# Edge weights of a graph layer: one 128-row product a tile with a zero-padded map, in place of pairs of 64-row products

## The chip, the cores and the metric

One Trainium2 chip, one of its cores. The metric is the device time of one launch in microseconds (us); lower is better. TensorE (PE) does the matrix products and its weight loads (PEld), VectorE (DVE) and ScalarE (ACT) the elementwise work, GpSimd (POOL) issues the gathers, SyncE (SP) issues loads and stores.

## The reference, cut to what matters

A graph layer with 12,500 nodes of 160 numbers (64 scalars and 32 vectors of 3) and 400,000 edges sorted by their target node. The part around the change:

```python
hid = jax.nn.silu(edge_scalars @ fc_w1 * _inv(R))      # (400000, 64) @ (64, 64)
w = hid @ fc_w2 * _inv(FC_HID)                         # (400000, 64) @ (64, 224)
w1, w2, w3, w4, w5 = jnp.split(w, [64, 128, 160, 192], axis=-1)
es, ev = h_s[edge_src], h_v[edge_src]                  # gather by source node
m_s1 = w1 * es * e0
m_v1 = (w2 * es)[:, :, None] * e1[:, None, :]          # and three more products
agg = jax.ops.segment_sum(mid, edge_dst, num_segments=n) * inv_nn
```

Every edge thus gets 224 weights from its 64 hidden numbers, these multiply the gathered source node, and the results are summed over the edges of each target. Two linear maps, a gate, a residual and a layer norm over the nodes follow. All is float32.

## The kernel before, in words

A first stage writes the mapped nodes to a table in HBM (`h_tab`) and prepares constants. Then the edges are taken in tiles of 128: 3125 tiles, in chunks of 20. The ten first tiles of a chunk lie on partitions 0 to 63 of the loaded edge data `es`, the ten others on partitions 64 to 127; the code calls these the two halves. `quads` cuts a chunk into five steps of four tiles, two of each half, so that there are 782 steps in all.

The main loop (L607 to L631) is unrolled, and its order on each engine is the order in which the program is written. One step n does this:

- `hide(n + 1)` (L608): in three steps of five, PE makes the hidden layer of the next tiles with a block-diagonal 128x128 map (L290), and ACT applies the SiLU (L292). The rows of `hid` again hold the two halves.
- `gather` (L299): POOL issues four indirect DMAs, one a tile, into a tile `hg`, of which there are four.
- `weights` (L311): PE makes the 224 weights of each of the four tiles into `pw`, with the tile's slice of `hid` as the stationary and `w2` as the moving operand. A tile of half 0 uses rows 0 to 63 of both, one of half 1 rows 64 to 127, and the loop takes them alternately.
- `products` (L319, and L328 three times): DVE multiplies `pw` by `hg` into `pr`, of which there are two.
- `add_up` and `add` (L387): DVE adds an earlier block's result into the accumulator. `choose` (L338, L341): DVE builds a selection tile every 1.25 steps.
- `go_on` does one piece of the finishing work on nodes that are complete (L394 to L437; the transposes L406 are PE's).
- `now`: pieces kept from the step before, either four transposes (L369) with two copies by ACT (L370), or eleven products (L378) with one copy (L382).
- `sum_up` of step n - 1 (L357): PE sums its `pr` by target, 16 products of 128x32 stationary columns, four side by side on the columns of the array. When two blocks are full, ACT copies them out (L361).

A product in float32 appears as two MATMUL records, each with its own weight load, so the four products of `weights` are eight records. PE signals DVE, ACT and SP through one semaphore, which the last record of each group raises. `w2` is built in the first stage: L235 to L242.

```python
    w2 = consts.tile([2 * S, NWT], F32, name="w2")
...
        for t in sorted(range(n), key=lambda t: (slots[t][1], slots[t][0])):
            half, c = slots[t]
            r = slice(half * S, (half + 1) * S)
            nc.tensor.matmul(pw[:, t, :NWT], hid[r, c * P:(c + 1) * P], w2[r],
                             start=True, stop=True)
```

Of the kernel before, what the change touches and what calls it, by code (L numbers as in the profile page):

```python
# [10 lines left out]
F32 = mybir.dt.float32  # L11
# [9 lines left out]
P = 128  # L21
S = 64
# [14 lines left out]
NWT = 224  # L37
# [19 lines left out]
def place_of(part, piece):  # L57

    first, step, count = SUMS[part]
    at = [first + a * step[0] + b * step[1] for a in range(count[0]) for b in range(count[1])]  # L60
    return at.index(PIECE[piece])
# [3 lines left out]
def gnn_kernel(  # L65
# [21 lines left out]
    nc = tc.nc  # L87
# [8 lines left out]
    consts = ctx.enter_context(tc.tile_pool(name="consts", bufs=1))  # L96
# [12 lines left out]
    for i in range(2):  # L109
        r = slice(S + i * V, S + (i + 1) * V)  # L110
# [31 lines left out]
    with tc.tile_pool(name="nodes", bufs=2) as nodes, tc.tile_pool(  # L142
        name="nodes_ps", bufs=8, space=PSUM
    ) as nps:
        CH = 4 * U * P
        for c0 in range(0, N, CH):
# [13 lines left out]
            for u in range(-(-cq // P)):  # L160
# [4 lines left out]
                for q in range(quarters):  # L165
                    r = slice(q * V, (q + 1) * V)
# [3 lines left out]
            for q in range(quarters):  # L170
                t = c0 // P + q * U
# [5 lines left out]
            if cn > full * P:  # L177
                n = cn - full * P
                t = c0 // P + full
# [52 lines left out]

    w1 = block_diagonal("w1", fc_w1, 2, 1.0)

    w2 = consts.tile([2 * S, NWT], F32, name="w2")  # L235
    for half in range(2):
        r = slice(half * S, (half + 1) * S)
        at_c = 0
        for c0, c1 in ((64, 128), (0, 64), (192, 224), (160, 192), (128, 160)):
            nc.scalar.dma_start(w2[r, at_c:at_c + c1 - c0], fc_w2[:, c0:c1])  # L240
            at_c += c1 - c0
    nc.vector.tensor_scalar_mul(w2, w2, 1.0 / math.sqrt(64))  # L242

# [19 lines left out]
    for to, part, pieces, w, r0, c0, by in maps:  # L263
        for k, piece in enumerate(pieces):
            half, at_p = divmod(place_of(part, piece), 3)
            m = terms.setdefault((to, part, half), len(terms))
            at_r = at_p * V
            r = l2[at_r:at_r + V, m, c0:c0 + w.shape[1]]
# [32 lines left out]
                in_offset=bass.IndirectOffsetOnAxis(ap=i, axis=0))  # L301
        return hg

    def weights(psum, hid, slots):

        pw = psum.tile([P, Q, 256], F32, name="pw")
        n = len(slots)
        for t in sorted(range(n), key=lambda t: (slots[t][1], slots[t][0])):
            half, c = slots[t]
            r = slice(half * S, (half + 1) * S)  # L310
            nc.tensor.matmul(pw[:, t, :NWT], hid[r, c * P:(c + 1) * P], w2[r],  # L311
                             start=True, stop=True)
        return pw

    def products(pool, pw, hg, n, between=()):

        pr = pool.tile([P, Q, NPR], F32, name="pr")

        nc.vector.tensor_mul(  # L319
            pr[:, :n, 6 * V:10 * V].rearrange("p t (k c) -> p t k c", k=2),  # L320
            pw[:, :n, :2 * S].rearrange("p t (k c) -> p t k c", k=2),
            hg[:, :n, None, :S].to_broadcast([P, n, 2, S]))
        for f in between:
            f()

        for k, (first, step) in enumerate(((1, 2), (4, -2), (10, 1))):
            full = pr[:, :n, first * V:]
            nc.vector.tensor_mul(  # L328
                bass.AP(tensor=full.tensor, offset=full.offset,
                        ap=[full.ap[0], full.ap[1], [step * V, 3], [1, V]]),  # L330
                pw[:, :n, None, 2 * S + k * V:2 * S + (k + 1) * V].to_broadcast([P, n, 3, V]),
                hg[:, :n, S:].rearrange("p t (i c) -> p t i c", i=3))
        return pr
# [51 lines left out]
    def add(base, os, b):  # L385
        window = acc[:, :, ds(base, W)]
        nc.vector.tensor_add(window, window, os[:, :, b])  # L387
# [66 lines left out]
    with tc.tile_pool(  # L454
        name="fin", bufs=1
    ) as fin, tc.tile_pool(name="edge", bufs=2) as edge, tc.tile_pool(
        name="deep", bufs=4
    ) as deep, tc.tile_pool(name="pw_ps", bufs=2, space=PSUM) as pw_ps, tc.tile_pool(
        name="pa_ps", bufs=2, space=PSUM
# [13 lines left out]
        def index(t):  # L473
            return group(t // GT)[0][:, t % GT:t % GT + 1]


        chunks = [((c, SIDE), (c + SIDE, SIDE)) for c in range(0, NB * TB - 2 * SIDE + 1, 2 * SIDE)]
# [8 lines left out]
        ess, hids = {}, {}  # L486

        def hide(n):

            if n >= len(steps):  # L490
                return
            c, i, _ = steps[n]
            if i % 2:
                return
            edges = [(t * P, m) for t, m in chunks[c]]
            if i == 0:
                ess[c] = load_hidden(loads, edges)
            hids[c, i // 2] = hidden(edge, misc_ps, ess[c], edges, 2 * i, 4)
# [104 lines left out]
        with tc.manual_schedule(engines={ENG.PE, ENG.DVE, ENG.Activation, ENG.Pool}):  # L603
            hide(0)
            before = None
            pieces = list(range(0, N, CHN))
            for n, (c, i, tiles) in enumerate(steps):  # L607
                hide(n + 1)  # L608
                hg = gather(deep, [index(t) for t, _, _ in tiles])
                now, later = later, []  # L610
                pw = weights(pw_ps, hids[c, i // 2], [(half, u - i // 2 * 4) for _, half, u in tiles])
                ready = []
                pr = products(edge, pw, hg, len(tiles), [lambda: ready.extend(add_up(1))])
                for a in ready:
                    add(*a)

                need = [b for m, b in order if m <= n]
                todo = [b for _, b in order if b not in sels]
                for b in need:
                    choose(b)  # L620
                order = [(m, b) for m, b in order if b not in need]
                if not need and order and order[0][0] <= n + 2:
                    choose(order.pop(0)[1])
                go_on()
                for f in now:
                    f()
                if before is not None:
                    sum_up(*before)
                before = (tiles, pr)
                if n % 30 == 6 and pieces:  # L630
                    self_connection(pieces.pop(0))  # L631
            assert not pieces
            sum_up(*before)
            while later:
                later.pop(0)()
            while adds:
                for a in add_up(1):
                    add(*a)
            while doing or to_do:
                go_on()  # L640
# [4 lines left out]
        with tc.For_i(0, n_redo, 1):  # L645
            n_again = nc.values_load(again[0:1, 0:1], min_val=0, max_val=G)
            sides = [(0, 3), (3, 2)]
            with tc.For_i(0, n_again, 1) as g, tc.For_i(0, BG, 1) as k:
                b = g * BG + k
                idx = loads.tile([P, TB], I32, name="idx1", bufs=1)  # L650
                nc.sync.dma_start(idx, src[ds(g, 1), :, ds(k * TB, TB)].rearrange("o p t -> p (o t)"))
                eat = loads.tile([P, TB, 4], F32, name="eat1", bufs=1)
                nc.sync.dma_start(eat, ea[ds(g, 1), :, ds(k * TB, TB)].rearrange("o p t k -> p (o t) k"))
                ends = loads.tile([1, 2], I32, name="ends1", bufs=1)
                nc.sync.dma_start(ends, bounds[:, ds(b, 1)].rearrange("k o -> o k"))
                edges = [(b * EB + t * P, m) for t, m in sides]
                es = load_hidden(loads, edges)
                hid = hidden(edge, misc_ps, es, edges, 0, 4)
                prs = {}
                for slots in quads([m for _, m in sides]):  # L660
                    hg = gather(deep, [idx[:, sides[h][0] + u:sides[h][0] + u + 1] for h, u in slots])
                    pr = products(edge, weights(pw_ps, hid, slots), hg, len(slots))
                    for slot, (h, u) in enumerate(slots):
                        prs[sides[h][0] + u] = pr[:, slot]
                r = edge.tile([P, TB], F32, name="r", bufs=1)
                nc.vector.tensor_scalar_add(r, rel[:, ds(b * TB, TB)], -float(W))
                first = nc.values_load(ends[0:1, 0:1], min_val=0, max_val=N - 1)
                last = nc.values_load(ends[0:1, 1:2], min_val=0, max_val=N - 1)
                with tc.For_i(first + W, last + 1, W) as base:
                    base = nc.s_assert_within(  # L670
                        base, 0, N - 1, skip_runtime_bounds_check_because="it is at most `last`")
                    sel = select(edge, r, eat)
                    pa = cleared(pa_ps)
                    for t in range(TB):
                        add_tile(pa[:, 0], sel, t, prs[t], start=False, stop=(t == TB - 1))
                    tt = edge.tile([V3, 2, 4, NO, W], F32, name="tt", bufs=1)
                    turned(misc_ps, copied(edge, pa, 1), 1, tt, 0)
                    add(base, second(edge, misc_ps, tt, 1), 0)
                    nc.vector.tensor_scalar_add(r, r, -float(W))
            for job in jobs:  # L680
                for f in finish(fin, misc_ps, *job):
                    f()
# [46 lines left out]
```

## Time and profile before

| what | us |
|---|---|
| median of 3 runs | 5778.92 (5755.6 to 5812.79) |
| the profiled execution | 5669.53 |
| its span, first to last instruction | 5667.7 |
| PE busy | 4182.8 (74%) |
| POOL busy | 3051.9 (54%) |
| DVE busy | 2642.3 (47%) |
| PEld busy | 2227.6 (39%) |
| ACT busy | 809.3 (14%) |
| mean granted TensorE clock | 0.816 of full |

The main loop runs from 114.9 us to 5626 us and looks the same in every slice. PE's busy time is no measure of full use: the ends of its matmuls are modelled and contain the latency of each. An idle engine is told in the profile by what ended its idle time ("<-"); "issue" means that no wait is seen, "remote" that a semaphore was awaited whose source the profile could not place.

### The profile page before, as it was taken

Reading aid. Unit: us, or ns where it says so; the run is one execution under the profiler, and the core shown is the slowest. Engines: PE = TensorE matmul, PEld = TensorE weight load, DVE = VectorE, ACT = ScalarE, POOL = GpSimd, SP = SyncE. Lnnn points to the kernel's source line nnn. Section 1 sums busy time; section 2 is a strip of 40 time slices with the busy share of each in tenths; the row PEclk is TensorE's granted clock in tenths of the full one; section 3 lists DMA queues with packets and bytes.
Section 4 is the critical chain, followed back from the end, with each engine's and each line's share of the span. In section 5 each row is a group of like instructions: output and inputs, shape, how many; then the busy total and the mean of one; then the engine's idle time right before and its main releaser. Section 6 shows DMA issues by size and latency. Waiting matters only on the chain.

```text
span 5667.7 us, 89792 instructions
## 1 busy us (share of the span) xinstructions
PE 4182.8 (74%) x36179; PEld 2227.6 (39%) x36179; DVE 2642.3 (47%) x5628; ACT 809.3 (14%) x1639; POOL 3051.9 (54%) x3134
## 2 busy tenths in 40 slices
PE   6777777767777767777777777777776767777776
PEld 5334433333344434334333333433333433434343
DVE  4444444444444444444444444444444444444444
ACT  0111111111111111111111111111111111111111
POOL 3555555555555555555555555555555555555553
PEclk7788887888888878888888788887887888888787
DMA  6222222222222222222222222222222322232221
GB/s 172 68 72 73 72 72 66 73 74 65 76 76 67 74 68 74 74 70 74 72 74 73 63 76 69 73 77 68 75 72 63 82 67 73 71 79 69 68 69 46
DMA packets 232392, 416.39 MB, mean 73 GB/s; under 512 B 64580, under 2 KB 160592, under 8 KB 231713
## 3 DMA queue, kind: packets, MB, share of 16 engines
q0 software_dynamic: 150000, 256.20, 17.3%
q1 hardware_dynamic: 65972, 142.43, 9.9%
q10 hardware_dynamic: 15994, 11.93, 0.8%
q8 instruction: 285, 4.67, 0.3%
q14 instruction: 141, 1.16, 0.1%
HBM read 394.32 MB, written 16.00 MB: 72 GB/s over the span
## 4 chain that ended last, share of the span: by engine, by line
PE 31%; another core or an unknown queue 8%; issue 6%; DVE 3%; ACT 3%; DVEq 0%; DMA 0%; POOL 0%; ACTq 0%; POOLq 0%
PE pa L357 13%; PE pw L311 6%; PE ph L290 4%; PE po L378 3%; PE pt L369 2%; DVE pr L328 2%; ACT tt L370 1%; PE pa L348 1%; ACT hid L292 1%; DVE pr L319 0%; PE pp L406 0%; PE psc L510 0%; ACT L292 0%; DVEq L582 0%
## 5 line engine op out<-in xcount | busy, mean ns | idle before, releaser
L299 POOL DMA_INDIRECT hg<-h_tab,idx x3125 | 3029.5, 969 | 2562.8 <-DVE pr L328 962.0
L357 PE MATMUL pa<-pr,sel 128*32 128x192 f32 x25000 | 1813.8, 395 | 312.7 <-issue 298.8
L319 DVE TENSOR_TENSOR pr<-pw,hg 128x512 f32<-128x512 f32 x782 | 539.1, 689 | 2648.7 <-remote 1400.2
L357 PEld LDWEIGHTS pa<-pr,sel 128*32 128x32 f32 x25000 | 888.3, 127 | 1060.3 <-issue 768.8
L328 DVE TENSOR_TENSOR pr<-pw,hg 128x384 f32<-128x384 f32 x2346 | 1158.2, 549 | 5.7 <-issue 4.9
L311 PE MATMUL pw<-w,hid 64*128 64x224 f32 x6250 | 990.0, 429 | 48.3 <-issue 38.8
L369 PE MATMUL pt<-ident,sa 128*96 128x128 f32 x1250 | 317.8, 344 | 814.6 <-ACT tt L370 418.6
L311 PEld LDWEIGHTS pw<-w,hid 64*128 64x128 f32 x6250 | 645.2, 219 | 585.8 <-issue 530.2
L341 DVE TENSOR_TENSOR sel<-oh,eat 128x640 f32<-128x640 f32 x625 | 517.8, 828 | 168.2 <-PE pw L311 51.2
L290 PE MATMUL ph<-es,w 128*128 128x512 f32 x940 | 552.0, 673 | 10.8 <-issue 8.3
L369 PEld LDWEIGHTS pt<-ident,sa 128*96 128x96 f32 x1250 | 124.7, 144 | 1000.5 <-ACT tt L370 496.0
L361 ACT COPY sa<-pa 128x384 f32<-128x384 f32 x313 | 149.5, 478 | 2085.0 <-PE pa L357 1042.7
L292 ACT ACTIVATE hid<-ph 128x512 f32<-128x512 f32 (+1 forms) x470 | 247.0, 526 | 1242.9 <-PE ph L290 855.1
L378 PE MATMUL po<-tt,l 96*96 96x256 f32 (+1 forms) x1738 | 401.7, 383 | 9.6 <-issue 8.7
L378 PEld LDWEIGHTS po<-tt,l 96*96 96x96 f32 x1738 | 274.5, 164 | 127.1 <-issue 47.6
L370 ACT COPY tt<-pt 96x256 f32<-96x256 f32 x626 | 229.3, 366 | 588.0 <-PE pt L369 361.1
L290 PEld LDWEIGHTS ph<-es,w 128*128 128x128 f32 x940 | 165.8, 219 | 198.1 <-issue 184.7
L406 PE MATMUL pp<-ident,acc 96*128 96x96 f32 x196 | 44.9, 325 | 239.6 <-DVE acc L387 218.9
L338 DVE TENSOR_TENSOR oh<-rel,iota 128x160 f32<-128x160 int16 x625 | 196.3, 314 | 0.0
L382 ACT COPY os<-po 96x512 f32<-96x512 f32 (+1 forms) x79 | 45.6, 577 | 714.9 <-PE po L378 485.1
L387 DVE TENSOR_TENSOR acc<-acc,os 96x64 f32 x625 | 132.7, 212 | 12.6 <-ACT os L382 7.9
L406 PEld LDWEIGHTS pp<-ident,acc 96*128 96x128 f32 x196 | 23.8, 170 | 273.3 <-issue 187.5
(61 smaller groups left out, 794.7 us busy)
## 6 DMA issues: line engine op xcount, KB each, us to landing
es<-in_es_t_dram SPq DMA_DIRECT2D x312, 320.0 KB
hg<-h_tab,idx POOLq DMA_INDIRECT x3125
h_tab<-ht ACTq DMA_DIRECT2D x8, 960.0 KB
xt<-in_x_dram SPq DMA_DIRECT2D x24, 320.0 KB
out_dram<-y SPq DMA_DIRECT2D x24, 320.0 KB
eat<-in_ea_dram SPq DMA_DIRECT2D x25, 250.0 KB
xv<-in_xv_t_dram SPq DMA_DIRECT2D x25, 187.5 KB
xs<-in_xs_t_dram SPq DMA_DIRECT2D x25, 125.0 KB
```

Source lines behind the costliest of these rows:

```text
L290: nc.tensor.matmul(ph[:k, c], w1[:k, :k], es[:k, t0 * P + c0 * P:t0 * P + c1 * P], start=True, stop=True)
L292: nc.scalar.activation(hid[:k, c], ph[:k, c], AF.Silu, scale=1.0 / math.sqrt(64))
L299: nc.gpsimd.indirect_dma_start(out=hg[:, t, :], out_offset=None, in_=h_tab, in_offset=bass.IndirectOffsetOnAxis(ap=i, axis=0))
L311: nc.tensor.matmul(pw[:, t, :NWT], hid[r, c * P:(c + 1) * P], w2[r], start=True, stop=True)
L319: nc.vector.tensor_mul(pr[:, :n, 6 * V:10 * V].rearrange("p t (k c) -> p t k c", k=2), pw[:, :n, :2 * S].rearrange("p t (k c) -> p t k c", ...
L328: nc.vector.tensor_mul(bass.AP(tensor=full.tensor, offset=full.offset, ap=[full.ap[0], full.ap[1], [step * V, 3], [1, V]]), pw[:, :n, None ...
L338: nc.vector.tensor_tensor(oh, r[:, :, None].to_broadcast([P, TB, W]), iota[:, None, :].to_broadcast([P, TB, W]), op=OP.is_equal)
L341: nc.vector.tensor_mul(sel, oh[:, :, None, :].to_broadcast([P, TB, 4, W]), e[:, :, :, None].to_broadcast([P, TB, 4, W]))
L357: nc.tensor.matmul(pa[k * W:(k + 1) * W], sel[:, t, k], a, start=start, stop=stop)
L369: nc.tensor.transpose(pt[:, half, b], sa[:, b, half * V3:(half + 1) * V3], ident)
L370: nc.scalar.copy(tt[:, half, :, at_b:at_b + nb].rearrange("c k b n -> c b k n"), pt[:, half, :nb].rearrange("c b (k n) -> c b k n", k=4))
L378: nc.tensor.matmul(po[:, k, :nb], l2[:, terms[to, part, half]], tt[:, half, part, :nb], start=(n == 0), stop=(n == len(of) - 1))
```

## The change

`w2` becomes two maps side by side, each of 128 rows: in the first, rows 64 to 127 are zero, in the second rows 0 to 63. Each tile's product now takes all 128 rows of its `hid` slice, both halves, against the map in which the other half's rows are zero. In the last chunk, where a column of `hid` has only half 0, it takes rows 0 to 63. The number of instructions in the main loop, their order, and what they wait for are the same on all five engines; the setup gains one memset and its scaling covers 448 columns in place of 224.

```diff
-    w2 = consts.tile([2 * S, NWT], F32, name="w2")
+    w2 = consts.tile([2 * S, 2, NWT], F32, name="w2")
+    nc.vector.memset(w2, 0.0)
     for half in range(2):
         r = slice(half * S, (half + 1) * S)
...
-            nc.scalar.dma_start(w2[r, at_c:at_c + c1 - c0], fc_w2[:, c0:c1])
+            nc.scalar.dma_start(w2[r, half, at_c:at_c + c1 - c0], fc_w2[:, c0:c1])
...
-    def weights(psum, hid, slots):
+    def weights(psum, hid, slots, filled):
...
-            r = slice(half * S, (half + 1) * S)
-            nc.tensor.matmul(pw[:, t, :NWT], hid[r, c * P:(c + 1) * P], w2[r],
+            r = slice(0, 2 * S) if c < filled else slice(0, S)
+            nc.tensor.matmul(pw[:, t, :NWT], hid[r, c * P:(c + 1) * P], w2[r, half],
                              start=True, stop=True)
...
-                pw = weights(pw_ps, hids[c, i // 2], [(half, u - i // 2 * 4) for _, half, u in tiles])
+                pw = weights(pw_ps, hids[c, i // 2], [(half, u - i // 2 * 4) for _, half, u in tiles],
+                             chunks[c][1][1] - i // 2 * 4)
...
-                    pr = products(edge, weights(pw_ps, hid, slots), hg, len(slots))
+                    pr = products(edge, weights(pw_ps, hid, slots, 2), hg, len(slots))
```

## The prediction

> **What bounds the kernel now.** I read the page's busy lines first, then the costliest groups, then the waits, then the timeline of one stretch. No engine is full: POOL 54%, DVE 47%. PE shows 74%, but that holds latencies. The span less the first stage, (5626 - 115) / 782, is 7.05 us a step. A step of POOL alone is four gathers at 0.95 us and 0.30 between them, 5.0 us; of DVE 2642.3 / 782 = 3.4 us. So the loop is bound by engines waiting in turn, and the question is whether `pw` (L311) lies in that ring. From the page's groups and from the waits:
>
> ```profile
> L299 POOL DMA_INDIRECT hg<-h_tab,idx x3125 | 3029.5, 969 | 2562.8 <-DVE pr L328 962.0
> L319 DVE TENSOR_TENSOR pr<-pw,hg 128x512 f32<-128x512 f32 x782 | 539.1, 689 | 2648.7 <-remote 1400.2
> L311 PE MATMUL pw<-w,hid 64*128 64x224 f32 x6250 | 990.0, 429 | 48.3 <-issue 38.8
> L369 PE MATMUL pt<-ident,sa 128*96 128x128 f32 x1250 | 317.8, 344 | 814.6 <-ACT tt L370 418.6
> ```
>
> ```profile
> DVE pr L319 <- remote: 1400.2, 267, 19.1
> POOL hg L299 <- DVE pr L328: 962.0, 291, 7.6
> DVE pr L319 <- PE pw L311: 784.7, 285, 10.1
> DVE pr L319 <- PE pa L357: 260.4, 51, 8.2
> ```
>
> Nearly all of DVE's idle time stands before L319, and L319 waits for the gathers, for `pw`, and through PE's semaphore for the release of a `pr`. POOL in turn waits for DVE to give an `hg` back. The timeline shows which is late:
>
> ```profile
> 3034.50 1.32 POOL L299 DMA_INDIRECT hg<-h_tab,idx  x1 [0.30 <-issue]
> 3035.16 1.03 PE L311 MATMUL pw<-w,hid 64*128 64x224 f32 x8
> 3036.12 4.99 PE L378 MATMUL po<-tt,l 96*96 96x256 f32 x22
> 3039.88 0.95 POOL L299 DMA_INDIRECT hg<-h_tab,idx  x1 [0.30 <-issue]
> 3041.43 0.69 DVE L319 TENSOR_TENSOR pr<-pw,hg 128x512 f32<-128x512 f32 x1 [5.48 <-PE po L378]
> ...
> 3043.90 1.03 PE L311 MATMUL pw<-w,hid 64*128 64x224 f32 x8
> 3044.86 0.53 PE L357 MATMUL pa<-pr,sel 128*32 128x192 f32 x8
> 3044.97 0.69 DVE L319 TENSOR_TENSOR pr<-pw,hg 128x512 f32<-128x512 f32 x1 [0.73 <-PE pw L311]
> ```
>
> The reader is to see two kinds of step. At 3043.90 the products start as the last pass of `pw` ends: `pw` is the late one. At 3035.16 `pw` ends at 3036.19, its gathers landed before, and DVE still waits 5.2 us: PE's semaphore arrives late. Followed step by step over the trace (start of L319 less end of the last L311), 274 of 781 steps start within 0.25 us of the end, 148 within 0.25 to 1.25 us, and 359 later. The late ones have a pattern: they come while POOL issues gathers and just after a dense burst of PE records. With POOL idle around it no PE signal is late; after the 32 records of L357 and then L311, with POOL busy, four of five are, by 2 to 4 us on average; after L290, which puts two records into 1 us, about one in ten. It behaves like a backlog that drains slowly. I don't know what it is, only when it comes.
>
> **What the skill says.** "TensorE: Matmul & The Clock Gate", Part 3, says that products of small contraction on different row groups run at the same time, and that one with few rows takes as long as one with all. The trace agrees:
>
> ```profile
> 3026.39 1.86 PE L311 MATMUL pw<-w,hid 64*128 64x224 f32 x8
> 3029.70 1.12 PE L290 MATMUL ph<-es,w 128*128 128x512 f32 x2
> 3030.76 1.03 PE L311 MATMUL pw<-w,hid 64*128 64x224 f32 x8
> 3036.12 4.99 PE L378 MATMUL po<-tt,l 96*96 96x256 f32 x22
> ```
>
> L378 runs one pass after the other: (4.99 - 0.38 for the last) / 21 = 0.219 us for 256 columns, or 0.19 us for 224. Eight passes of L311 in single file would take 8 x 0.19 = 1.52 us and an end of 0.27; 1.03 us is 4 x 0.19 + 0.27. The pairs do overlap fully. "TensorEngine Tiling (Array Packing)", Key Properties, says that a change of tiling drains the array. The trace agrees in kind: the L290 at 3029.70 has two 512-column passes, 2 x 0.43 = 0.86 us, and L311 starts 1.06 us after it, so 0.2 us is lost to the first weight load and the change of shape. The forecast goes by both.
>
> **The change part by part.**
>
> *Single file.* Each step's `pw` gains 4 x 0.19 = 0.75 us at full clock. The granted clock here is either full or half. At half, L311 takes 1.86 us at 3026.39, and the gain is 1.5. The passes run from 346 to 741 ns with median 349 and mean 429, so (429 - 349) / 349 = 23% of them are at half clock. Mean: 0.77 x 0.75 + 0.23 x 1.5 = 0.92 us; over 781 steps 720 us of PE time.
>
> *Shape changes.* `pw` now has the full-row shape of L290 before it in 469 steps (938 passes of L290, two a group), and of L369 or L378 after it in 313 + 79 steps. There the weights can load under the product before and nothing drains: bounded by 0 and 0.2 us a boundary; I take 0.2 before and 0.15 after, 94 + 59 = 150 us. The changes to and from L357 stay. Net PE time: 570 us, and 720 if nothing is saved.
>
> *Records.* Eight MATMUL and eight loads as before, in twice the time. No new wait on any queue, and none queued behind one; DVE, ACT, POOL and SP get the same lists.
>
> *Setup.* One memset of 128x448 on DVE: a memset of 96x1056 takes 0.94 us in the trace, so 0.4 us, at about 1.5 us, where DVE next waits for DMAs (idle 2.9 us). ACT's loads of `w2` start at 35 us, long after. The scaling grows from 0.25 to about 0.5 us at 63 us, before a DVE wait of 5.7 us for a DMA. Taken as nothing; without that cover, under 1 us.
>
> *How much of the 570 is on the path.* This is where I choose. Low bound: in a step whose signal is late by more than the gain, DVE starts when the backlog has drained, and a `pw` that takes longer with the same number of records gives it time to drain, so DVE sees nothing. Taking in every step only what the gain exceeds the lateness gives 336 of a gross 749 us (each step at its own clock), 45%. High bound: the chain. In the stretch from 3000 to 3060 us it runs through PE most of the time (L357 32.1%, L311 18.0%, L290 9.5%), because PE's own order puts L357, L290 and the next `pw` behind this one; then nearly all is exposed. PE does have slack: 814.6 us before L369 and 239.6 before L406. I take 55%: 570 x 0.55 = 315 us. What hides the rest is the late signal; were it gone, all 570 would show.
>
> *Clock.* A full-row pass works twice as many rows. Over the trace's 3.4 us clock stretches, the clock drops to half after those with little array work (columns x rows x stationary columns) and returns after those with much; the level between, about 2650 of 8192 full-clock array cycles, sorts some 95% of them. With the work of `pw` doubled in place, the stretches above it rise from 63% to 70%: 0.07 x 5510 = 386 us of time would go from half to full clock. That saves up to half of what PE works in it; at 0.35 us per us and 55% exposed, some 70 us. Bounds: 0 and 135.
>
> Sum: 315 - 70 = +245 us. On the profiled execution 5669.5 + 245 = 5915 us. The median of the three runs lies 109 us (1.9%) above that execution, so I put the same increment on the median: 5779 + 245 = 6024, stated as 6020.
>
> **The rivals.**
>
> - *PE is the whole path (0.20).* Everything adds: 570 to 720 us, centre 6350. For it: the chain. Against it: the 814.6 us of PE idle before L369 and the 359 late steps.
> - *Absorbed (0.14).* The extra passes lie in the time that DVE waits for late signals and POOL for buffers: within 1%, 5780. For it: DVE's 1400.2 us of "remote". Against: 274 steps have no lateness at all.
> - *The clock carries it (0.15), on the other side.* If the denser array holds the full clock nearly throughout, each of the some 185 half-clock steps gets back 1.1 us on L357 (2.3 against 1.2 us of starts for its 32 passes), 0.8 on the old `pw` and some 0.5 on the rest, 2.4 us or 440 us; 70% exposed it is -310 us, against a cost that then has no half-clock part, 0.55 x (781 x 0.75 - 150) = 240: 70 us faster, 5710. It decides where the mean granted clock passes about 0.93. Against it: the in-place count gives 70% of stretches, or 0.85.
> - *The change does not do what it says:* if full-row passes still overlapped, the time would fall by the 150 us of boundaries. L378 and L290 go in single file, so I give this nothing of its own; the rival before it holds its range.
>
> **How the numbers follow.** The likeliest case, partly exposed, has 0.51; its own range is +110 to +400 us, 5890 to 6180. Slower by over 1% is that case and the first rival, 0.71; within 1% (about what a measurement of this kernel can tell from no change) 0.14; faster 0.15. The range leaves out half of the faster case and the upper end of the first rival: 5730 to 6330.
>
> **What would show it.** After: L313 in 128*128 form, eight passes in about 1.78 us at full clock; its start about 0.86 us after a 512-column L291 at full clock; L321's idle time with "PE pw" growing by about 0.3 us a step and "remote" shrinking; POOL's wait for L330 growing by about the added time; clock 0.83 to 0.86. Wrong if `pw` groups stay near 1.03 us, if the clock goes over 0.93, or if "remote" falls by far more than the growth in "PE pw", which would mean that late signals hang on the shape of `pw` and not on the burst before it.

## The result, and the profile after

| kernel | median, us | runs | profiled execution, us | mean granted clock |
|---|---|---|---|---|
| before | 5785.34 (5755.6 to 5817.4) | 20 | 5669.53 | 0.816 |
| after | 5805.97 (5790.48 to 5828.53) | 20 | 5798.33 | 0.870 |

The ratio is 1.0034, 95% interval 1.0018 to 1.0051: 10 to 30 us slower, where 245 us were forecast. The likeliest case was wrong; what came is, for the larger part, the rival "Absorbed". The groups of `pw` take longer, as was expected; the rest of PE's work gets shorter at the higher clock, and of what remains hardly anything shows in the time.

The two profiles can't be laid side by side as they are: the profiled execution of before lay 2% under its own median, that of after lay on it. The 129 us between the spans are therefore not the change. The page of after, busy times and groups:

```profile
PE 4414.6 (76%) x36179; PEld 2830.2 (49%) x36179; DVE 2649.1 (46%) x5629; ACT 807.5 (14%) x1639; POOL 3050.2 (53%) x3134
...
L300 POOL DMA_INDIRECT hg<-h_tab,idx x3125 | 3027.8, 969 | 2690.8 <-DVE pr L330 1073.5
L359 PE MATMUL pa<-pr,sel 128*32 128x192 f32 x25000 | 1679.4, 377 | 282.0 <-issue 276.7
L321 DVE TENSOR_TENSOR pr<-pw,hg 128x512 f32<-128x512 f32 x782 | 540.0, 691 | 2796.2 <-remote 1372.0
L313 PE MATMUL pw<-w,hid 128*128 128x224 f32 x6250 | 1490.5, 384 | 34.0 <-issue 28.1
...
L371 PE MATMUL pt<-ident,sa 128*96 128x128 f32 x1250 | 296.8, 325 | 752.1 <-ACT tt L372 432.7
```

and its waits:

```profile
DVE pr L321 <- remote: 1372.0, 234, 19.3
...
POOL hg L300 <- DVE pr L330: 1073.5, 307, 8.7
...
DVE pr L321 <- PE pw L313: 879.1, 336, 11.2
```

L313 is in its 128-row form and its busy time half as long again; each wait shown and each row of another engine stands within some 12% of its partner of before. PE's busy time as a whole grows by less than L313 does, by 232 us, from 4182.8; one of the rows that shrank is L359, whose partner of before was

```profile
L357 PE MATMUL pa<-pr,sel 128*32 128x192 f32 x25000 | 1813.8, 395 | 312.7 <-issue 298.8
```

Two steps from the timeline of after:

```profile
3032.95 1.68 PE L313 MATMUL pw<-w,hid 128*128 128x224 f32 x8
...
3034.66 0.69 DVE L321 TENSOR_TENSOR pr<-pw,hg 128x512 f32<-128x512 f32 x1 [2.01 <-PE pw L313]
...
3036.39 1.12 PE L291 MATMUL ph<-es,w 128*128 128x512 f32 x2
...
3037.35 1.68 PE L313 MATMUL pw<-w,hid 128*128 128x224 f32 x8
...
3044.55 0.69 DVE L321 TENSOR_TENSOR pr<-pw,hg 128x512 f32<-128x512 f32 x1 [6.41 <-remote]
```

The group takes 1.68 us instead of 1.03. In the first step DVE starts 0.03 us after the group's end, so in this step all of the longer group is on DVE's path. In the second the group ends at 3039.03 and DVE starts 5.5 us later; there DVE can hardly see 0.65 us more or less at PE. L313 starts 0.96 us after L291, where its partner started 1.06 us after L290. Step by step over the trace, 354 of 781 steps start within 0.25 us of the end of `pw` (before 274) and 326 later than 1.25 us (before 359).

The runs below were made in five sets, each with its own runs of the kernel before, and that kernel took 4218 and 4222 us in the first and the last set and 5660, 5787 and 5788 us in the three between; so ratios hold within a set only. What differs in the traces is the subject of the experiments: in the first and last set no PE semaphore that could be matched to its group came later than 0.2 us after the group's end ("on time"), in the sets between, and in both profiles above, many did ("late"; their lateness sums to some 4400 us over the trace of before and 4500 us over that of after, as far as the signals, of which some 5% are missing from these two traces, can be matched to their groups).

### The profile page after: what moved, and what is told of

It is laid out like the page before. It is cut to its first block, busy times and chain, and to the rows that moved or that the text cites. A ratio compares the mean times of both kernels' runs of the same rounds, so it can differ in the third digit from the quotient of the medians.

```text
span 5796.5 us, 89793 instructions
## 1 busy us (share of the span) xinstructions
PE 4414.6 (76%) x36179; PEld 2830.2 (49%) x36179; DVE 2649.1 (46%) x5629; ACT 807.5 (14%) x1639; POOL 3050.2 (53%) x3134
## 4 chain that ended last, share of the span: by engine, by line
PE 34%; another core or an unknown queue 8%; issue 4%; ACT 3%; DVE 2%; DVEq 0%; DMA 0%; ACTq 0%
PE pa L359 13%; PE pw L313 10%; PE ph L291 4%; PE po L380 3%; PE pt L371 2%; DVE pr L330 1%; ACT tt L372 1%; ACT hid L293 1%; PE pa L350 1%; ACT sa L363 0%; PE psc L512 0%; PE pp L408 0%; ACT L293 0%; DVE pr L321 0%
## 5 line engine op out<-in xcount | busy, mean ns | idle before, releaser
L300 POOL DMA_INDIRECT hg<-h_tab,idx x3125 | 3027.8, 969 | 2690.8 <-DVE pr L330 1073.5
L359 PE MATMUL pa<-pr,sel 128*32 128x192 f32 x25000 | 1679.4, 377 | 282.0 <-issue 276.7
L321 DVE TENSOR_TENSOR pr<-pw,hg 128x512 f32<-128x512 f32 x782 | 540.0, 691 | 2796.2 <-remote 1372.0
L313 PE MATMUL pw<-w,hid 128*128 128x224 f32 x6250 | 1490.5, 384 | 34.0 <-issue 28.1
L313 PEld LDWEIGHTS pw<-w,hid 128*128 128x128 f32 x6250 | 1276.8, 209 | 393.3 <-issue 347.2
L359 PEld LDWEIGHTS pa<-pr,sel 128*32 128x32 f32 x25000 | 846.1, 122 | 934.0 <-issue 696.0
L330 DVE TENSOR_TENSOR pr<-pw,hg 128x384 f32<-128x384 f32 x2346 | 1159.9, 550 | 6.2 <-issue 5.4
L371 PE MATMUL pt<-ident,sa 128*96 128x128 f32 x1250 | 296.8, 325 | 752.1 <-ACT tt L372 432.7
L291 PE MATMUL ph<-es,w 128*128 128x512 f32 x940 | 529.9, 647 | 12.4 <-issue 7.4
L380 PE MATMUL po<-tt,l 96*96 96x256 f32 (+1 forms) x1738 | 396.5, 378 | 17.9 <-issue 16.7
L380 PEld LDWEIGHTS po<-tt,l 96*96 96x96 f32 x1738 | 278.8, 163 | 114.0 <-issue 33.8
L291 PEld LDWEIGHTS ph<-es,w 128*128 128x128 f32 x940 | 161.4, 213 | 196.8 <-issue 183.2
```

The source lines that it names most:

```text
L291: nc.tensor.matmul(ph[:k, c], w1[:k, :k], es[:k, t0 * P + c0 * P:t0 * P + c1 * P], start=True, stop=True)
L300: nc.gpsimd.indirect_dma_start(out=hg[:, t, :], out_offset=None, in_=h_tab, in_offset=bass.IndirectOffsetOnAxis(ap=i, axis=0))
L321: nc.vector.tensor_mul(pr[:, :n, 6 * V:10 * V].rearrange("p t (k c) -> p t k c", k=2), pw[:, :n, :2 * S].rearrange("p t (k c) -> p t k c", ...
L330: nc.vector.tensor_mul(bass.AP(tensor=full.tensor, offset=full.offset, ap=[full.ap[0], full.ap[1], [step * V, 3], [1, V]]), pw[:, :n, None ...
L359: nc.tensor.matmul(pa[k * W:(k + 1) * W], sel[:, t, k], a, start=start, stop=stop)
L371: nc.tensor.transpose(pt[:, half, b], sa[:, b, half * V3:(half + 1) * V3], ident)
```

## The experiments

**The products of a half in turn.** The sort now puts the two products of one half next to each other. It was made to take the pairs apart without a change of shape.

```diff
-        for t in sorted(range(n), key=lambda t: (slots[t][1], slots[t][0])):
+        for t in sorted(range(n), key=lambda t: (slots[t][0], slots[t][1])):
```

> The kernel before with the two tiles of half 0 ahead of the two of half 1, so that the 64-row products go in single file and hardly overlap, with no zero rows, no denser array and no change of shape saved. Theory 1 (absorbed: the time is set by late PE signals during the gathers, and the longer edge weights lie beside): within 1% of before, 5730 to 5840 us. Theory 2 (cancelled: the longer PE time costs some 250 us or more, and the changed kernel gets it back from the clock and the shape changes): 6030 to 6190 us. In both, a group of eight passes takes about 1.6 to 1.7 us at full clock and the granted clock stays near 0.82.

Measured, on time: 4221.29 us against 4218.03, ratio 1.0004 [0.9992, 1.0016]. But its timeline shows that the premise failed:

```profile
3032.90 1.03 PE L311 MATMUL pw<-w,hid 64*128 64x224 f32 x8
```

The group still takes 1.03 us. The eight passes start in pairs, 13 ns apart (7 ns before), the pairs 183 to 293 ns apart, though two products of one half now follow each other in the program. So PE seems to have taken up the other half's products ahead of them (the trace shows neither the half of a pass nor the order in which the passes were queued; in program order the group would take some 1.5 us, an estimate: six gaps of 0.19 us and the last pass's 0.35 us). This run therefore says nothing about single file, and is in effect a second profile of the kernel before, with signals on time; its groups:

```profile
L299 POOL DMA_INDIRECT hg<-h_tab,idx x3125 | 3069.6, 982 | 1092.1 <-issue 973.3
...
L319 DVE TENSOR_TENSOR pr<-pw,hg 128x512 f32<-128x512 f32 x782 | 539.3, 690 | 1390.8 <-DMA hg<-h_tab,idx 789.2
```

POOL issues its gathers back to back ("issue", mostly the 0.30 us between two, is 973.3 of its 1092.1 us of idle time), 3125 of them 1.25 us apart, 3.9 ms of the 4.2. With signals on time the gathers are the pace.

The same kernel in a late set:

> The kernel of halves_in_turn once more, since its first run fell where PE's signals are on time and the gathers set the pace (before 4218 us). If the signals are late this time (before near 5660 to 5790 us): theory 1 (the longer weights lie beside late signals) says within 1% of before; theory 2 (cost cancelled by the denser array's higher clock, which this kernel lacks) says 4 to 7% slower. If they are on time again: ratio 1.000, as before.

5791.25 us against 5787.13, 1.0002 [0.9983, 1.0021], groups of 1.03 us again. It serves below as a profile of the old form whose span (5779.6 us) does lie at its median.

**The change twice over, to see where PE becomes the bound.** Every product of the changed kernel is made twice into the same place, eight more passes or 1.5 us a step.

```diff
-            nc.tensor.matmul(pw[:, t, :NWT], hid[r, c * P:(c + 1) * P], w2[r, half],
-                             start=True, stop=True)
+            for _ in range(2):
+                nc.tensor.matmul(pw[:, t, :NWT], hid[r, c * P:(c + 1) * P], w2[r, half],
+                                 start=True, stop=True)
```

> The changed kernel with each edge-weight product issued twice (the second overwrites the first with the same values): 1.5 us of full-row PE work more in each step, 32 PE records in place of 16. Theory 1: up to 150 us more than the changed kernel, at most 5950 us, since PE's own work at full clock, about 6 us a step, still fits into the 7.05 us. Theory 2: 0.55 x 781 x 1.5 = 640 us more less some 100 us for the clock, about 6350 us.

On time: 5309.21 us, 1.2584 [1.2564, 1.2603], and nearly the whole idle time of the products is `pw`:

```profile
DVE pr L322 <- PE pw L314: 2437.5, 775, 15.0
```

PE is busy for 93% of the span at a clock of 0.968: with the gathers no longer the pace, PE is. (Neither range of the expectation, made for late signals, applies here.)

> The kernel of full_twice once more. With signals on time it took 5309 us, 1.258 of before, PE 93% busy. With late signals: theory 1 says that 1.5 us of PE work more a step is again partly beside, and the dense burst before the signal is followed by a longer, sparser stretch, so it loses much less than 26%: 1.00 to 1.10 of before, at most 6300 us. Theory 2: 1.10 to 1.15 and up.

Late: 6063.24 us, 1.0474 [1.0439, 1.0509]. Eight more passes at 0.19 us are 781 x 1.51 = 1180 us; the clock rises from 0.865 to 0.944 and shortens other work, so that PE's busy time grows by 817 us (4420.0 in `after_third`, 5236.8 here). The time rises by 265 us over the 5798.43 us of the changed kernel in the same set. Where PE's signals are late, two thirds of even this are not seen.

**The weights one step ahead.** `pw` of step n + 1 is made before the products of step n wait, so that DVE finds it ready; once with pairs, once with full rows.

```diff
-                hide(n + 1)
+                hide(n + 2)
...
-                pw = weights(pw_ps, hids[c, i // 2], [(half, u - i // 2 * 4) for _, half, u in tiles])
+                pw, pws[n + 1] = pws.pop(n), weigh(n + 1)
```

> The kernel before with the edge weights and the hidden layer made one step earlier, so that PE's signal for a step's weights is one step old when DVE needs it. Nothing is left out. Theory 1: lateness of that signal no longer holds DVE, and the time falls well below before, to some 4800 us (as a bound, the 1530 us that DVE waits for weights that are already made would go: 4250). Theory 2: PE's own order is the path, and the time stays within 3% of before, 5600 to 5950 us.

> The changed kernel with the same shift by one step as in the run ahead_pairs. Theory 1: as fast as ahead_pairs within 2% as long as the gathers set the pace; slower than it by up to 400 us (0.5 us of PE a step) if PE sets it. Theory 2: within 1% of ahead_pairs, as the cost and the clock cancel there as well.

On time: 4184.28 us, 0.9922 [0.9905, 0.9940], and 4187.93 us, 0.9924 [0.9907, 0.9940]. With `pw` made a step ahead, full rows and pairs cost the same, and both gain 0.8%. The signals being on time, these two runs say nothing about what lateness costs. In a late set:

> The kernel of ahead_full once more (changed kernel, weights one step earlier). With signals on time it took 0.992 of before. With late signals: theory 1 says that the lateness of the weights' own signal is taken off DVE, some 1000 us or more, 4600 to 5000 us where before takes 5700; theory 2 says no more than 3% off.

5675.53 us, 0.9824 [0.9789, 0.9860]: a gain, but not the one expected. DVE hardly waits for `pw` any more (120.8 us are left) and instead waits for other late signals:

```profile
DVE pr L321 <- remote: 1009.5, 206, 19.4
...
DVE pr L321 <- PE pa L359: 616.0, 187, 9.0
```

**Both kernels again, unchanged.**

> The kernel before itself, for a trace beside that of the changed kernel in the same condition: ratio 1.00. If PE signals are on time, DVE's waits before L319 are for the landing of gathers and not 'remote', POOL's starts are 1.25 us apart nearly throughout, and no step has a signal later than 0.2 us; if they are late, the picture of the first profile, near 5785 us.

> The changed kernel itself once more, to have it beside a run of the kernel before whose PE signals are on time (before took 4218 us in the runs of the first set, with no late PE signal in their traces, against 5785 us where its own profile was taken). Theory 1, now: the pace is set beside PE, by POOL's gathers where the signals are on time (4 x 1.25 us a step, 3.94 ms in all) and by the late signals where they are not, so the changed kernel is within 0.7% of before in either condition. Theory 2 (cost cancelled by the clock): with the signals on time the clock is higher before the change already (0.91 in the run with the halves in turn), little is left to gain, and the PE time shows: 3 to 6% slower, 4340 to 4470 us where before takes 4218.

> The changed kernel a third time. Late signals: ratio 1.003, as twice before. Signals on time: theory 1 says within 0.7% of before, because four gathers take 5.0 us a step and PE's work with full rows about as much; theory 2 says 3 to 6% slower.

Before against itself 0.9991 [0.9975, 1.0007]; after 1.0035 [1.0013, 1.0057] and 1.0018 [1.0006, 1.0030]. The change costs 0.2 to 0.4% in late sets. The set on time that the expectation of `after_again` hoped for did not come.

**One gather in four.** POOL gathers only the first tile of each step, and the products of all four read it: three quarters of the gathered data are left out. DVE and PE do as much as before.

```diff
-        for t, i in enumerate(idx):
+        for t, i in enumerate(idx[:1]):
...
-            hg[:, :n, None, :S].to_broadcast([P, n, 2, S]))
+            hg[:, :1, None, :S].to_broadcast([P, n, 2, S]))
...
-                hg[:, :n, S:].rearrange("p t (i c) -> p t i c", i=3))
+                hg[:, :1, S:].rearrange("p t (i c) -> p t i c", i=3).to_broadcast([P, n, 3, V]))
```

> The kernel before with one gather a step in place of four; all four tiles are multiplied by the first tile's rows, so three quarters of the gathered data are left out. POOL then needs 1.25 us a step. Theory 1: the gathers were the pace, so the time falls, to what DVE and PE need: 3.4 us a step of DVE, some 4 us of PE, 3200 to 3600 us. Theory 2: PE is the path already, and the time falls by less than 5%.

> The changed kernel with one gather a step in place of four, as in one_gather_pairs. Theory 1: with the gathers out of the way PE is the path and the price of the single file shows: 250 to 500 us slower than one_gather_pairs. Theory 2: equal to one_gather_pairs within 1.5%, since clock and shape changes pay for it there as well.

In a set where before took 5659.88 us: pairs 3741.88 us, 0.6616 [0.6597, 0.6636], longer than the 3200 to 3600 us expected; full rows 4130.04 us, 0.7296 [0.7274, 0.7318]. Two things follow. The late signals go: one of the nearly 3000 matched PE semaphores comes later than 0.5 us. And the change now costs 388 us, 0.50 us a step. The wait of the products for `pw` with pairs,

```profile
DVE pr L319 <- PE pw L311: 887.4, 549, 5.9
```

and with full rows:

```profile
DVE pr L321 <- PE pw L313: 1275.4, 724, 12.3
```

The difference of these two lines, 388.0 us, is the difference of the times. Here, and only here, is DVE's wait for `pw` the change's price one for one; PE is busy for 89 and 90% of these spans.

**Single file without full rows.** To replace the run whose premise had failed: all four products take rows 0 to 63.

```diff
-            r = slice(half * S, (half + 1) * S)
+            r = slice(0, S)
```

> All four products of a step take rows 0 to 63 (the weights of the second half's tiles are computed from the first half's hidden numbers, so a part of the computation is changed), so no two can run side by side: the eight passes go in single file as in the changed kernel, while the rows worked and the change of tile shape at every boundary stay as before. First, the group is 1.6 to 1.8 us at full clock against 1.03, or the premise fails. Absorbed (the longer weights lie in time that is lost anyway): within 0.5% of before, clock 0.80 to 0.83. Paid by the clock (single file costs, and the higher clock of the full rows gives it back): slower than before by 1.5 to 5%, at a clock of 0.80 to 0.83, while the changed kernel was at 1.003. If the set has signals on time, where before takes 4218 us, absorbed gives within 0.5% as well.

> The same single file of 64 rows, with one gather in four (three quarters of the gathered data left out), where PE sets the pace and every step's price shows. The pairs took 3741.88 us and the full rows 4130.04 us. If single file alone is the price, 781 steps at 0.65 us give +508 us: 4250 us, and the changed shape and clock then give 120 us back in the full-row form. If the boundaries give nothing back, about 4130 us; if they give back the 150 us that the forecast took, about 4280 us.

Both fell into a set with signals on time. `same_rows`: 4370.62 us against 4221.57, 1.0363 [1.0339, 1.0387], at a clock of 0.939. `one_gather_same`: 4347.52 us. Now the passes do go in single file, as its timeline shows:

```profile
2502.39 1.78 PE L311 MATMUL pw<-w,hid 64*128 64x224 f32 x8
2504.10 4.99 PE L378 MATMUL po<-tt,l 96*96 96x256 f32 x22
```

The price with one gather in four splits. The first two of these three were measured in another set, but none of them has late signals:

| one gather in four | us | group of `pw`, mean us | clock |
|---|---|---|---|
| pairs of 64 rows | 3741.88 | 1.04 | 0.951 |
| full rows, single file | 4130.04 | 1.74 | 0.970 |
| 64 rows, single file | 4347.52 | 1.83 | 0.935 |

Single file costs 606 us (0.785 us x 781 = 613 by the groups), not the 508 expected, which took the group's growth from the full-row form. Full rows then give 217 us back, more than the 120 to 150 expected. At full clock the full-row group is 0.10 us shorter (1.677 for 1.777, its first load no longer shows), 78 us; and it has lost the 0.093 us of the change of shape at 930 boundaries, 86 us. The other some 50 us fit the higher clock, which was not isolated.

With four gathers and signals on time the single file of `same_rows` costs 149 us of these 606: neither nothing, as "absorbed" expected, nor the whole. DVE's waits are then shared between the gathers and `pw`:

```profile
DVE pr L319 <- PE pw L311: 1259.1, 613, 6.9
...
POOL hg L299 <- issue: 961.7, 2848, 94.2
```

**What makes PE's signals late?** My theory was a dense burst of PE records (the 32 of L357) while POOL gathers. The first kernel halves the burst: in all but the closing tile of a sum, two of the four products are left out.

```diff
-        for k, (first, step, count) in enumerate(SUMS):
+        for k, (first, step, count) in enumerate(SUMS if stop else SUMS[:2]):
```

> The kernel before with two of the four column products of each tile's sum left out (all four are kept in the one tile in ten that closes a pair of blocks), so that the burst after each step's weights has about 35 records in place of 64; two thirds of the sums are missing in the output. Same gathers. Theory A (a PE signal is late when gathers and a dense PE burst meet): far fewer and shorter late signals, and the time falls by well over 10% where before takes some 5700 us. Theory B (the gathers alone delay PE's signals): lateness and time stay within 5% of before. Where the signals are on time anyway: within 1% of before, as the gathers set the pace.

Late: 5508.13 us against 5788.38, 0.9518 [0.9484, 0.9551], at the edge of the 5% that the other theory allowed, and the sum of the lateness does not fall: some 5400 us. The burst is not the main cause.

The next two change how far POOL may run ahead (`name="deep", bufs=4` to 2 and to 8):

> The kernel before with two gather buffers in place of four. Theory A with a ring (signals are freed when POOL's run of gathers ends, then 2.2 us of products, then the next run): 5.0 + 2.2 us a step do not hang on the number of buffers, and the time stays within 3% of before where signals are late. Rival (the four buffers are used up by latency): over 8% slower in either condition.

> The kernel before with eight gather buffers in place of four. Theory A with a ring: within 3% of before, since POOL is then only further ahead and still gives way only when it waits. Rival (POOL's waits for a buffer, 962 + 535 us in the profile, are what holds the loop): 5% or more faster.

1.0006 [0.9990, 1.0021] and 1.0020 [1.0003, 1.0038]: the number of `hg` does not matter. The last one adds a third `pr` to the kernel with the weights ahead, in pairs, so that no product has to wait for the release of a `pr`:

```diff
-        pr = pool.tile([P, Q, NPR], F32, name="pr")
+        pr = pool.tile([P, Q, NPR], F32, name="pr", bufs=3)
```

> The kernel before with the weights one step earlier, as in ahead_pairs, and three product buffers in place of two, so that neither the weights' signal nor that of the sums two steps back is awaited when it is fresh. Theory A: DVE's waits for late PE signals shrink by over half; where signals are late the time falls by 5 to 20% below before; on time: the gathers' pace, within 1% of 0.992 of before.

5990.11 us, 1.0342 [1.0297, 1.0386], slower where a gain was expected. The waits went elsewhere once more:

```profile
ACT hid L292 <- remote: 1407.4, 167, 34.2
...
DVE sel L341 <- PE pa L357: 1124.0, 213, 12.8
```

Where the late signals that were covered had stood, others stand. Why the time rose is not shown.

## Why the prediction was wrong, step by step

**What bounds the kernel.** Waits in turn with PE's signals late: seen again in every trace of a late set with all four gathers. The ring's pace of 7.05 us a step stays unexplained. A sign that PE's work does not set it was on the page: the slack before L369, 814.6 us, is 150.9 us in `one_gather_same`, where PE does set the pace.

**Single file, +720 us: right in kind, and at full clock in size.** Eight passes 189 ns apart, 1.777 us on 64 rows against 1.03 in pairs, the 0.75 us forecast. The mean group went from 1.314 to 1.940 us, 782 x 0.625 = 489 us. This holds already the first weight load that no longer shows (the second pass starts after 189 ns, not 293) and fewer groups at half clock (some 100 for 185), where the forecast had kept 23% of the passes at half clock. Single file alone was 606 us at a clock of 0.935. "TensorE: Matmul & The Clock Gate" of the Trainium skill, by which the forecast went, held: 64 rows take as long as 128 (189 ns each), which stands there under "Why this matters for your kernels" rather than in Part 3; and products on separate row groups run side by side, as Part 3 says, here in pairs 7 ns apart.

**Shape changes, -150 us: right.** L290 to L311 lost 95 ns at full clock, L291 to L313 loses 2; L369 and L378 after it the same (93 to 2 ns), while the boundaries with L359 keep their 95. That is 86 us at 930 boundaries (I had counted 861 and the first load at part of them), and with the first load, 0.10 us x 781 = 78, 164 us. The sign named for it, 0.86 us from L291 to L313, came out as 0.96: the first weight load still shows between L291's own two passes (533 ns), and the step to L313 takes 429. The drain of "TensorEngine Tiling (Array Packing)" of the Trainium skill, Key Properties, which says that a change of tiling mode drains the array, has thus a price here: some 0.095 us.

**Records and setup: right.** The instruction counts differ by the one memset, which takes 0.43 us at 1.40 us.

**How much of the 570 is on the path: this step failed.** I put 55% on the path, 315 us, with 45% as the low bound. PE's busy time grew by 232 us over the profile of before and by 197 us over `halves_again`, a profile of the old form at its own median:

```profile
PE 4217.3 (73%) x36179; PEld 2250.4 (39%) x36179; DVE 2639.6 (46%) x5628; ACT 806.7 (14%) x1639; POOL 3063.8 (53%) x3134
```

Of these some 200 us, 10 to 30 us show, a tenth. At 55% it would have been 110 to 130 us (an estimate: 0.55 of 197 and of 232). The low bound rested on the thought that a step whose signal is on time shows its longer `pw`. Each such step does; but the ring then waits that much less somewhere else. The products' waits in `halves_again`:

```profile
DVE pr L319 <- remote: 1534.0, 280, 19.5
...
DVE pr L319 <- PE pw L311: 721.2, 268, 9.1
```

Against the two lines of after, 1372.0 and 879.1: 158 us more wait for `pw`, 162 us less "remote", sum 2255 before and 2251 after. In this pair the wait changed its name. Other profiles of late sets give the same picture: with pairs `hg_2` has 1466.1 and 763.8 and `hg_8` 1566.1 and 748.7, with full rows `after_third` 1356.2 and 961.4. The set in which both kernels were profiled as they stand shows it less cleanly: from `before_again` to `after_again` "remote" falls from 1322.8 to 1139.6, "PE pw" grows only from 795.2 to 876.9, and waits put down to the maps (L378, then L380) grow from 90.7 to 272.9. Both forms of "wrong" that the forecast named for this line were thus avoided, and it was wrong all the same: "PE pw" grows by 0.1 to 0.2 us a step (0.3 was forecast), and "remote" falls by 0.2. POOL's wait for L330 grows by some 65 us (1008.0 to 1073.5), not by the added time. The forecast had booked the growth of "PE pw" as cost and the shrinking of "remote" only as far as single steps were late.

**Clock, -70 us: right in direction, too small: the second term that failed.** The clock is either full or half here, so a mean of 0.816 is full for 63% of the time and one of 0.870 for 74%: some 600 us (0.11 of 5510) went from half to full clock, where 386 were forecast. By the forecast's own 0.35 us per us that is 210 us of PE time, not 135 at most. The trace agrees: 489 us for the groups less 86 for the boundaries less the 232 us that PE's busy time grew leaves 171 us that other PE work got shorter; L357's row alone, which kept its boundaries, lost 134.4 us. So 570 us of net PE work, less at most 135, came out as some 200, and this is about half of the miss; the share on the path is the other half. The clock and the boundaries did not pay for all of it, since PE was busy for some 200 us more and the time did not show them. Single file without full rows, with signals late, was not measured, so the split is by the counts of the traces.

**The rivals.** "Absorbed" (0.14) was right in the time, and for its reason in what the clock left: the waits above. "PE is the whole path" is right where one gather in four is left, 388 us, and with twice the products; it falls for the kernel as it is. "The clock carries it" needed 0.93 and got 0.87, and was right in that the clock pays a good third of the longer groups. "The change does not do what it says" is out by the 189 ns.

**What stays open.** Why PE's signals are late in some sets and not in others (the record gives the same chip number for the first set, on time, and the fourth, late), and what sets 7.05 us a step when they are. They need the gathers (gone with one in four, in a set that is otherwise late), halving the dense burst did not lessen them, and they don't depend on how many `hg` there are; DVE's and ACT's own signals came within 20 ns in 19 of 20 cases throughout. One rival was not tested: the recording itself. Every run's span and clock come from the profiler's records, and in late sets with four gathers over half of its semaphore records are lost: the trace of the same kernel holds 64077 semaphore updates on time (`halves_in_turn`) and 28009 late (`halves_again`), while with one gather in four a late set has nearly as many (28610) as one on time (29341). Whether late signals and lost records have one cause, and whether signals are late without a recording, no run shows. The changed kernel in its given order was not measured with signals on time; `same_rows` suggests a price there below 3.6%, if full rows give back a part as they do with one gather in four.

## What to carry to other kernels

A chain of waits that runs through an engine most of the time does not make its work the pace: before an operation's growth is put on the path, ask whether the ring has another wait beside it that shrinks by as much, and sum the two. Before that, look at whether the change shortens other work: here the clock took back a third of the cost. To know an operation's price, take away what covers it (here three gathers of four) and read the wait for it: 388 us bare, some 20 us where the clock and the other waits cover it. And look at an experiment's own timeline for its premise before its time is read; a changed order of instructions did not change what ran side by side.

## What was not expected of the hardware

- One program had two levels, 4218 and 5660 to 5788 us, set by set. In the late one a PE semaphore came up to several microseconds after the end of its group (over 6 us in some 7 of 100 in the trace of before), while DVE's and ACT's came within 20 ns, and this went with indirect gathers being issued. Over half of the semaphore records were missing from those traces (28009 for 64077 in one and the same kernel).
- Products of 64 rows, two of one half after two of the other in program order, ran in the same 1.03 us as in alternation, but took 1.78 us when all were on one half: it looks as if those of one half overtook those waiting for the other.
- The granted clock followed the rows worked, not only the time PE was busy: with one gather in four, single file of 64 rows had 0.935 with PE busy for 91% of the span, the same of 128 rows 0.970 with 90%; in the late sets it went from 0.816 to 0.870.
